# Softmax denominators of a causal attention: key blocks added by accumulating DMAs, one matmul pass of sums a unit

## The chip, the core and the metric

The kernel runs on one core of a Trainium2 chip. The metric is the device time of one execution in microseconds (us); lower is better. Engines: PE (TensorE) does matmuls, with its weight loads shown as PEld; DVE (VectorE), ACT (ScalarE) and POOL (GpSimd) do elementwise work and reductions; SP (SyncE) issues DMAs. POOL and ACT can issue DMAs too. Sixteen DMA engines move the data.

## The reference

Two residual blocks over x of 2 x 1024 tokens of 128 features, in float32. The first is causal attention with 8 query heads in 2 groups of 4, whose keys and values come from a latent of 32 per group. The second is a mixture of 32 small experts with a router. Cut to what matters:

```python
q = (xn @ wq).reshape(B, T, 2, 4, 128)
k_lat = (xn @ wk_down).reshape(B, T, 2, 32)
v_lat = (xn @ wv_down).reshape(B, T, 2, 32)
k = einsum('bkhl,ld->bkhd', k_lat, wk_up)
v = einsum('bkhl,ld->bkhd', v_lat, wv_up)
scores = einsum('bqhrd,bkhd->bhrqk', q, k) * 128 ** -0.5
scores = where(causal, scores, finfo.min)
probs = softmax(scores, axis=-1)
y = einsum('bhrqk,bkhd->bqhrd', probs, v).reshape(B, T, 1024) @ wo
x = x + layernorm(y)
x = x + layernorm(moe(layernorm(x)))
```

`moe` picks 2 of 4 expert groups for each token, then 6 experts in them, and adds a shared expert and a small anchor expert.

## The kernel before

*Attention.* Queries are multiplied by the key's up projection beforehand, so scores are products over 32 latent features, and the four heads of a group lie in the four groups of 32 partitions. The work is cut into 16 units (b, g, q): batch, group, block of `QC` = 256 queries; in order b, then q, then g. Unit q has q + 1 steps of 256 keys each (two key tiles of 128), 40 steps in all; the last step of a unit is the diagonal one (s == q), where the second key tile has only 128 queries. The main loop is in `attention()`. For step k it issues in this order:

- `numerators` (L533): scores s of the step in four PSUM banks, one for each head (L541); the maximum is subtracted by a further matmul (L555); then ACT writes the exponentials to the SBUF tile `pr` (L561: 128 keys x 4 heads x 512), and in the diagonal step POOL zeroes what lies above the diagonal (L564, affine_select). `pr` is one of three buffers with the tag "wide".
- `weigh` of the step before (k-1), which calls `values` (L574): o += v' pr on PE (L578), into the one accumulator bank with tag "o".
- `one_item`: a piece of the row maxima of a later unit, `maxima`: matmuls sm (L476, L486) in four PSUM banks and reductions on DVE (L493). Scores, maxima and the rest share seven banks that go round.
- `sums` of step k-1 (L584): a second pass of matmuls over the same `pr`, now with a matrix of ones (L587). It gives the softmax denominators in the other half of the accumulator bank. After a unit's last step ACT copies both halves to SBUF (`raw`, L594), and `normalized` divides on ACT and DVE, with a Newton step.

Between these, `tick()` lets one piece of the side work run: projections of the second batch, and `route(i)`, which takes 512 tokens whose units are normalized through the output projection, both layer norms and the router. PE, DVE, ACT, POOL and SP each run their instructions in exactly this program order.

*After attention.* `experts(0, 0)` runs all experts for the first 512 tokens. The other 1536 are sorted by expert group: POOL scatters their rows into DRAM by indirect DMAs (`placed`, L955), slots of 256 rows are worked off by `Slots.run`, and their outputs are scattered back (`results`, L1180). The experts' weights per token are spread over partitions by DMAs from DRAM (`spread_tile`, L1050, three buffers with a tag of their own; L1304 and L1310 for the first 512 tokens, issued on SP's queue).

Of the kernel before, what the change touches and what calls it, by code (L numbers as in the profile page):

```python
# [10 lines left out]
F32 = mybir.dt.float32  # L11
BF16 = mybir.dt.bfloat16
AF = mybir.ActivationFunctionType
ALU = mybir.AluOpType
# [11 lines left out]
def attn_moe_block(  # L26
# [19 lines left out]
    anchor_w_down: bass.AP,  # L46
    out: bass.AP,
):

# [64 lines left out]

    x_sb = [const.tile([P, NT, D], F32, name=f"x{b}") for b in range(B)]
    xr = [x[b].rearrange("(t p) d -> p t d", p=P) for b in range(B)]
    wq_sb = work.tile([P, NH, P], F32, tag="wide", name="wq_sb", bufs=3)
    wkup_sb = const.tile([L, P], F32, name="wkup_sb")  # L120
    wvup_sb = const.tile([L, P], F32, name="wvup_sb")
    wkd_sb = const.tile([P, G, L], F32, name="wkd_sb")
# [169 lines left out]
    def fold_queries():  # L292

        pt = bank("pt_up")
        nc.tensor.transpose(pt[:, 0:L], wkup_sb, ident[0:L, 0:L])
        nc.vector.tensor_copy(wkupT, pt[:, 0:L])
        wqT = work.tile([P, NH, P], F32, tag="wide", name="wqT", bufs=3)
        for g in range(G):
            heads = range(g * R, (g + 1) * R)
            pt = bank("pt_wq")  # L300
            for i, h in enumerate(heads):
                nc.tensor.transpose(pt[:, ts(i, P)], wq_sb[:, h, :], ident)
            nc.scalar.copy(wqT[:, g * R : (g + 1) * R, :].rearrange("p h d -> p (h d)"), pt)
            yield
        for g in range(G):
            pa = bank("pa")
            for i in range(R):
                nc.tensor.matmul(
                    pa[:, ts(i, L)], lhsT=wqT[:, g * R + i, :], rhs=wkupT, start=True, stop=True
                )  # L310
            nc.scalar.mul(aq[:, g, :], pa[:, 0 : R * L], scale)
            yield
# [219 lines left out]

    def numerators(u, s):  # L533

        b, g, q = u
        qT, kT, _ = qkv[b]
        banks = [bank(f"s{b}{g}{q}{s}") for _ in range(R)]
# [18 lines left out]
                dst, lhsT=ones[rows, :], rhs=less, start=False, stop=True, skip_group_check=True  # L556
            )
        tables(EXP_LN)
        pr = work.tile([P, R, 2 * QC], F32, tag="wide", name=f"pr{b}{g}{q}{s}", bufs=3)
        for r in range(R):  # L560
            nc.scalar.activation(pr[:, r, 0:m], banks[r][:, 0:m], AF.Exp)  # L561
        if s == q:
            own = pr.rearrange("p r (i c) -> p r i c", c=QC)[:, :, :, 0:P]
            nc.gpsimd.affine_select(  # L564
                out=own, in_=own, compare_op=ALU.is_ge, fill=0.0, base=0,
                pattern=[[0, R], [0, 2], [1, P]], channel_multiplier=-1,
            )
        return pr

# [1 line left out]

    ot = {}

    def values(u, s, pr, o):  # L574
        b, g, _ = u
        for kt, at, lo, n in pieces(u, s):
            for r in range(R):
                nc.tensor.matmul(  # L578
                    o[ts(r, L), lo : lo + n], lhsT=qkv[b][2][:, kt, ts(g, L)],
                    rhs=pr[:, r, at : at + n],  # L580
                    start=(kt == 0), stop=False, skip_group_check=True,
                )

    def sums(u, s, pr, o):  # L584
        for kt, at, lo, n in pieces(u, s):
            for r in range(R):
                nc.tensor.matmul(  # L587
                    o[ts(r, L), QC + lo : QC + lo + n], lhsT=ones32,
                    rhs=pr[:, r, at : at + n], start=False, stop=True, skip_group_check=True,
                )  # L590
        b, g, q = u
        if s == q:
            t = work.tile([P, 2 * QC], F32, tag="raw", name=f"raw{b}{g}{q}", bufs=3)
            nc.scalar.copy(t, o)  # L594
            ends.append(normalized(u, t))

    def normalized(u, t):

        b, g, q = u
        own, total = t[:, 0:QC], t[:, QC : 2 * QC]  # L600
        r = work.tile([P, QC], F32, tag="rsum", name=f"rsum{b}{g}{q}", bufs=2)
        tables(EXP_LN)
        nc.scalar.activation(r, total, AF.Ln)
        nc.scalar.activation(r, r, AF.Exp, scale=-1.0)
        yield HOP
        ot[u] = work.tile([P, QC], F32, tag="ot", name=f"ot{b}{g}{q}", bufs=NU + 2)
        nc.vector.scalar_tensor_tensor(total, total, -1.0, r, ALU.mult, ALU.mult)
        nc.vector.tensor_tensor(own, own, r, ALU.mult)
        nc.vector.scalar_tensor_tensor(ot[u], total, 2.0, own, ALU.add, ALU.mult)
        yield  # L610

    def attention():
# [31 lines left out]
        def weigh(entry):  # L644
# [3 lines left out]
            if s == 0:  # L648
                o[u] = acc(f"o{u[0]}{u[1]}{u[2]}")
            values(u, s, pr, o[u])  # L650

        for k, (u, s) in enumerate(steps):
            while done < need[k]:
# [8 lines left out]
            pr = numerators(u, s)  # L662
            if k > 5:
                tick()
            if waiting:
                weigh(waiting)
            turn_ready(ready)
# [4 lines left out]
                one_item()  # L672
            if k > 5:
                tick()
            if waiting:
                sums(*waiting, o[waiting[0]])
            waiting = (u, s, pr)
            tick()
            if any(need[j] - done > j - k - 1 for j in range(k + 1, len(steps))):
# [1 line left out]
                tick()  # L681
        weigh(waiting)
        sums(*waiting, o[waiting[0]])


    chosen = const.tile([P, NTS, NG], F32, name="chosen")
# [361 lines left out]
        return wb  # L1048

    def spread_tile(name):  # L1050
        return work.tile([P, NC * SL], F32, tag="spread", name=f"spread{name}", bufs=3)

    def quarter(name):
        return work.tile([P, QC], F32, tag="quarter", name=name, bufs=6)
# [183 lines left out]
    def finish(i):  # L1238
# [23 lines left out]
            tables(EXP_LN)  # L1262
        else:
            yield 4
        both = work.tile([P, R, 2 * QC], F32, tag="wide", name=f"y{i}", bufs=3)
        both = both.rearrange("p r c -> p (r c)")[:, 0 : n * TOPG * D]
        at = (i - ND) * TB
        nc.sync.dma_start(
# [160 lines left out]
```

## Time and profile before

| | us |
|---|---|
| timed runs of before, median of 3 | 460.58 (456.15 to 461.75) |
| profiled execution, time | 449.65 |
| profiled execution, span of its instructions | 448.0 |
| PE busy / DVE busy / ACT busy / POOL busy in the span | 402.7 / 293.2 / 220.5 / 117.5 |

The span is the time from the first to the last instruction of the profiled execution. Busy is time in which the engine has at least one instruction under way; a matmul in float32 appears as two records, and four matmuls in different quarters of the array run side by side, so a group's busy time is less than its count times its mean. A row of the page's groups gives line, engine, operation, output and input with shapes, the count, then busy time in us and the mean of one in ns, then the engine's idle time just before them and what ended it. A row of the waits gives who waited for whom: us in total, times, and the longest. In the windows, each engine's busy time stands in front of its number of instructions.

### The profile page before, as it was taken

Reading aid. Unit: us, or ns where it says so; the run is one execution under the profiler, and the core shown is the slowest. Engines: PE = TensorE matmul, PEld = TensorE weight load, DVE = VectorE, ACT = ScalarE, POOL = GpSimd, SP = SyncE. Lnnn points to the kernel's source line nnn. Section 1 sums busy time; section 2 is a strip of 40 time slices with the busy share of each in tenths; the row PEclk is TensorE's granted clock in tenths of the full one; section 3 lists DMA queues with packets and bytes.
Section 4 is the critical chain, followed back from the end, with each engine's and each line's share of the span. In section 5 each row is a group of like instructions: output and inputs, shape, how many; then the busy total and the mean of one; then the engine's idle time right before and its main releaser. Section 6 shows DMA issues by size and latency. Waiting matters only on the chain.

```text
span 448.0 us, 10253 instructions
## 1 busy us (share of the span) xinstructions
PE 402.7 (90%) x3727; PEld 253.8 (57%) x3727; DVE 293.2 (65%) x1001; ACT 220.5 (49%) x469; POOL 117.5 (26%) x296
## 2 busy tenths in 40 slices
PE   8997899999999999998998999998789999997820
PEld 4554445645555555644554544447678899986620
DVE  5469852687699789799872576597433555455734
ACT  3454376276343577565566556436323433333621
POOL 4000100020001212022001688525852334241130
PEclk9999999999999999999999999999989999999995
DMA  7888000000000620000000257677278667787221
GB/s 216 186 235 174 2 0 2 1 4 1 1 2 1 173 75 2 1 1 2 1 2 2 53 179 215 174 218 217 93 219 242 207 209 239 220 246 232 83 63 55
DMA packets 46419, 47.63 MB, mean 106 GB/s; under 512 B 21152, under 2 KB 39312, under 8 KB 46368
## 3 DMA queue, kind: packets, MB, share of 16 engines
q1 hardware_dynamic: 42960, 41.51, 33.0%
q0 software_dynamic: 2112, 4.18, 2.8%
q10 hardware_dynamic: 1296, 1.28, 0.9%
q8 instruction: 30, 0.49, 0.5%
q14 instruction: 21, 0.17, 0.1%
HBM read 38.12 MB, written 11.45 MB: 111 GB/s over the span
## 4 chain that ended last, share of the span: by engine, by line
PE 51%; DVE 22%; DMA 12%; issue 6%; ACT 5%; POOL 2%; SPq 1%; ACTq 0%; POOLq 0%; DVEq 0%
DVE nm L493 9%; PE sm L476 7%; PE s L541 5%; DMA got<-placed 5%; PE o L578 4%; PE pgs L1148 4%; PE o L587 3%; PE pus L1148 3%; PE ys L1171 3%; PE pp L429 3%; PE pg L1317 3%; DMA y<-results 2%; PE oacc L1331 2%; PE pu L1318 2%; PE po L712 2%
## 5 line engine op out<-in xcount | busy, mean ns | idle before, releaser
L493 DVE TENSOR_REDUCE nm<-sm 128x1 f32<-128x512 f32 (+2 forms) x192 | 92.7, 548 | 35.2 <-PE sm L486 24.1
L561 ACT ACTIVATE pr<-s 128x512 f32<-128x512 f32 (+1 forms) x160 | 75.6, 558 | 71.8 <-PE s L555 71.8
L564 POOL TENSOR_SCALAR_AFFINE_SELECT pr<-pr 128x1024 f32<-128x1024 f32 x16 | 18.1, 1130 | 185.9 <-ACT pr L561 185.9
L541 PE MATMUL s<-qT,kT 32*128 32x256 f32 (+1 forms) x640 | 51.1, 383 | 4.6 <-DVE nm L493 3.8
L1156 DVE TENSOR_TENSOR hids<-hids,pus 128x512 f32<-128x512 f32 x30 | 20.6, 687 | 46.4 <-PE pus L1148 44.1
L1171 PE MATMUL ys<-wd_sb,hids 128*128 x300 | 41.0, 276 | 7.1 <-DVE hids L1157 5.3
L1180 POOL DMA_INDIRECT results<-ys,to_row x30 | 31.5, 1049 | 59.6 <-ACT ys L1177 37.0
L476 PE MATMUL sm<-kT,qT 32*128 32x512 f32 (+3 forms) x384 | 46.4, 525 | 0.6 <-DVE nm L493 0.4
L1171 PEld LDWEIGHTS ys<-wd_sb,hids 128*128 128x128 f32 x300 | 40.0, 191 | 10.9 <-DVE hids L1157 6.3
L541 PEld LDWEIGHTS s<-qT,kT 32*128 32x128 f32 x640 | 33.6, 184 | 21.4 <-issue 9.8
L578 PE MATMUL o<-pr,v 128*32 128x256 f32 (+1 forms) x640 | 39.4, 364 | 1.0 <-POOL preceded L855 1.0
L587 PE MATMUL o<-pr,ones 128*32 128x256 f32 (+1 forms) x640 | 39.3, 363 | 0.0
L1148 PE MATMUL pgs<-hTp,wbs 128*128 128x256 f32 x120 | 32.0, 390 | 1.2 <-issue 1.2
L1148 PE MATMUL pus<-hTp,wbs 128*128 128x256 f32 x120 | 30.9, 380 | 0.0
L578 PEld LDWEIGHTS o<-pr,v 128*32 128x32 f32 x640 | 16.7, 109 | 22.4 <-issue 10.3
L587 PEld LDWEIGHTS o<-pr,ones 128*32 128x32 f32 x640 | 17.2, 109 | 20.0 <-issue 10.6
L1157 DVE TENSOR_TENSOR hids<-hids,spreads 128x512 f32<-128x512 f32 (+1 forms) x45 | 27.2, 604 | 1.6
L955 POOL DMA_INDIRECT placed<-rows,place_of x24 | 24.5, 1020 | 7.5 <-issue 4.5
L1155 ACT ACTIVATE hids<-pgs 128x512 f32<-128x512 f32 x30 | 17.9, 598 | 15.3 <-PE pgs L1148 15.3
L476 PEld LDWEIGHTS sm<-kT,qT 32*128 32x128 f32 x384 | 18.2, 183 | 12.4 <-issue 3.6
L1148 PEld LDWEIGHTS pus<-hTp,wbs 128*128 128x128 f32 x120 | 23.1, 192 | 3.2
L1148 PEld LDWEIGHTS pgs<-hTp,wbs 128*128 128x128 f32 x120 | 21.2, 195 | 5.0 <-issue 2.9
(303 smaller groups left out, 628.1 us busy)
## 6 DMA issues: line engine op xcount, KB each, us to landing
wbs<-wgu SPq DMA_DIRECT2D x15, 640.0 KB, 4.4
spreads<-cw_slot SPq DMA_DIRECT2D x30, 256.0 KB, 4.0
spreadd<-cw_rows SPq DMA_DIRECT2D x16, 256.0 KB
got<-placed SPq DMA_DIRECT2D x15, 180.0 KB, 3.7
placed<-zero SPq DMA_DIRECT2D x1, 2640.0 KB
wbd<-wgu SPq DMA_DIRECT2D x4, 640.0 KB, 7.2
spreads<-cw_slot SPq DMA_DIRECT2D x60, 32.0 KB, 3.5
y<-results SPq DMA_DIRECT2D x3, 512.0 KB, 3.7
```

Of the source, the lines that this page charges most:

```text
L476: nc.tensor.matmul(banks[r][:, at : at + k1 - k0], lhsT=qT[ts(r, L), g, ts(qt, P)], rhs=kT[ts(r, L), g, k0:k1], start=(at == 0), stop=Fals ...
L493: nc.vector.tensor_reduce(nm[:, k0 // BC, j, r : r + 1], banks[r][:, at : at + k1 - k0], AX.X, ALU.max, negate=True,)
L541: nc.tensor.matmul(banks[r][:, at : at + n], lhsT=kT[rows, g, ts(kt, P)], rhs=qT[rows, g, q * QC + lo : q * QC + lo + n], start=(i == 0), ...
L561: nc.scalar.activation(pr[:, r, 0:m], banks[r][:, 0:m], AF.Exp)
L578: nc.tensor.matmul(o[ts(r, L), lo : lo + n], lhsT=qkv[b][2][:, kt, ts(g, L)], rhs=pr[:, r, at : at + n], start=(kt == 0), stop=False, skip ...
L587: nc.tensor.matmul(o[ts(r, L), QC + lo : QC + lo + n], lhsT=ones32, rhs=pr[:, r, at : at + n], start=False, stop=True, skip_group_check=True,)
L955: move = nc.gpsimd.indirect_dma_start(out=placed[:, :], out_offset=bass.IndirectOffsetOnAxis(ap=place_of[:, k, t : t + 1], axis=0), in_=ro ...
L1148: nc.tensor.matmul(p[:, lo : lo + SL], lhsT=wb[:, m, ts(c, P)], rhs=hT, start=(lo == 0), stop=(c == pair[-1]), skip_group_check=True,)
L1156: nc.vector.tensor_tensor(hid[:, 0:n], hid[:, 0:n], up, ALU.mult)
L1157: nc.vector.tensor_tensor(hid[:, 0:n], hid[:, 0:n], sp[:, pair[0] : pair[-1] + 1, :].rearrange("p c t -> p (c t)"), ALU.mult,)
L1171: nc.tensor.matmul(o[:, ts(j, D)], lhsT=hid[:, at : at + P], rhs=w, start=(c == 0 and j == 0), stop=(c == NC - 1), skip_group_check=True,)
L1180: move = nc.gpsimd.indirect_dma_start(out=results[:, :], out_offset=bass.IndirectOffsetOnAxis(ap=self.to_row[i][:, j : j + 1], axis=0), in ...
```

## The change

For ten of the sixteen units (all with q > 0 except two of the last batch's second group: `by_dma`) the per-step pass of `sums` is dropped. Instead, the numerators of the unit's steps are added up in SBUF by DMAs that accumulate into their destination, issued on POOL's queue: `add_tiles` adds the first key tile's half of `pr` to the second's, `add_steps` adds the result of one step to that of the next. The matmul with ones then runs once a unit, over the total (`sums_at_once`), three steps after the unit's last one. For these additions `pr` is laid out by blocks of 128 queries: (block, head, query) instead of (head, block, query). The values' half of the accumulator is copied to SBUF as soon as the unit's last values are in, the sums' half after `sums_at_once`. The tag "wide" has six buffers instead of three, and the spread expert weights now take their buffers from it. After the change the accumulating DMAs are at L616, L618 and L623, the one pass of sums at L629, the two copies at L595 and L634, the exponentials at L565, affine_select at L570 and the values at L588.

```diff
@@ -116,7 +118,7 @@
-    wq_sb = work.tile([P, NH, P], F32, tag="wide", name="wq_sb", bufs=3)
+    wq_sb = work.tile([P, NH, P], F32, tag="wide", name="wq_sb", bufs=6)
...
@@ -556,14 +559,17 @@
                 dst, lhsT=ones[rows, :], rhs=less, start=False, stop=True, skip_group_check=True
             )
         tables(EXP_LN)
-        pr = work.tile([P, R, 2 * QC], F32, tag="wide", name=f"pr{b}{g}{q}{s}", bufs=3)
+        pr = work.tile([P, R, 2 * QC], F32, tag="wide", name=f"pr{b}{g}{q}{s}", bufs=6)
+        pr = pr.rearrange("p r c -> p (r c)").rearrange("p (k r c) -> p k r c", r=R, c=P)
         for r in range(R):
-            nc.scalar.activation(pr[:, r, 0:m], banks[r][:, 0:m], AF.Exp)
+            nc.scalar.activation(
+                pr[:, 0 : m // P, r, :], banks[r][:, 0:m].rearrange("p (k c) -> p k c", c=P), AF.Exp
+            )
         if s == q:
-            own = pr.rearrange("p r (i c) -> p r i c", c=QC)[:, :, :, 0:P]
+            own = pr[:, 0:3:2, :, :]
             nc.gpsimd.affine_select(
                 out=own, in_=own, compare_op=ALU.is_ge, fill=0.0, base=0,
-                pattern=[[0, R], [0, 2], [1, P]], channel_multiplier=-1,
+                pattern=[[0, 2], [0, R], [1, P]], channel_multiplier=-1,
             )
         return pr
 
@@ -571,33 +577,66 @@
 
     ot = {}
 
+    def by_dma(u):
+
+        return u[2] > 0 and not (u[0] == B - 1 and u[1] == G - 1 and (u[2] + 1) * QC % BC == 0)
+
     def values(u, s, pr, o):
-        b, g, _ = u
+        b, g, q = u
         for kt, at, lo, n in pieces(u, s):
             for r in range(R):
                 nc.tensor.matmul(
                     o[ts(r, L), lo : lo + n], lhsT=qkv[b][2][:, kt, ts(g, L)],
-                    rhs=pr[:, r, at : at + n],
+                    rhs=pr[:, at // P : (at + n) // P, r, :],
                     start=(kt == 0), stop=False, skip_group_check=True,
                 )
+        if s == q and by_dma(u):
+            t = raw[u] = work.tile([P, 2 * QC], F32, tag="raw", name=f"raw{b}{g}{q}", bufs=3)
+            nc.scalar.copy(t[:, 0:QC], o[:, 0:QC])
+
+    raw = {}
 
     def sums(u, s, pr, o):
         for kt, at, lo, n in pieces(u, s):
             for r in range(R):
                 nc.tensor.matmul(
                     o[ts(r, L), QC + lo : QC + lo + n], lhsT=ones32,
-                    rhs=pr[:, r, at : at + n], start=False, stop=True, skip_group_check=True,
+                    rhs=pr[:, at // P : (at + n) // P, r, :], start=False, stop=True,
+                    skip_group_check=True,
                 )
         b, g, q = u
         if s == q:
             t = work.tile([P, 2 * QC], F32, tag="raw", name=f"raw{b}{g}{q}", bufs=3)
             nc.scalar.copy(t, o)
-            ends.append(normalized(u, t))
-
-    def normalized(u, t):
-
+            ends.append(normalized(u, t[:, 0:QC], t[:, QC : 2 * QC]))
+
+    def add_tiles(u, s, pr):
+
+        if s < u[2]:
+            nc.gpsimd.dma_start(out=pr[:, 2:4], in_=pr[:, 0:2], accum_op=ALU.add)
+        else:
+            nc.gpsimd.dma_start(out=pr[:, 2], in_=pr[:, 1], accum_op=ALU.add)
+
+    def add_steps(u, s, pr, last):
+
+        own = pr[:, 2:4] if s < u[2] else pr[:, 0:3:2]
+        nc.gpsimd.dma_start(out=own, in_=last[:, 2:4], accum_op=ALU.add)
+
+    def sums_at_once(u, pr):
         b, g, q = u
-        own, total = t[:, 0:QC], t[:, QC : 2 * QC]
+        o = bank(f"sums{b}{g}{q}")
+        for r in range(R):
+            nc.tensor.matmul(
+                o[ts(r, L), 0:QC], lhsT=ones32, rhs=pr[:, 0:3:2, r, :], start=True, stop=True,
+                skip_group_check=True,
+            )
+        t = raw.pop(u)
+        nc.scalar.copy(t[:, QC : 2 * QC], o[:, 0:QC])
+        ends.append(normalized(u, t[:, 0:QC], t[:, QC : 2 * QC]))
+
+    def normalized(u, own, total):
+
+        b, g, q = u
         r = work.tile([P, QC], F32, tag="rsum", name=f"rsum{b}{g}{q}", bufs=2)
         tables(EXP_LN)
         nc.scalar.activation(r, total, AF.Ln)
@@ -648,6 +687,26 @@
             if s == 0:
                 o[u] = acc(f"o{u[0]}{u[1]}{u[2]}")
             values(u, s, pr, o[u])
+            if by_dma(u):
+                add_tiles(u, s, pr)
+
+        past = []
+
+        def add_past():
+
+            if not past:
+                return
+            u, s, pr = past[-1]
+            if by_dma(u) and s > 0:
+                assert past[-2][0:2] == (u, s - 1)
+                add_steps(u, s, pr, past[-2][2])
+
+        def sum_past():
+
+            if len(past) > 1:
+                u, s, pr = past[-2]
+                if by_dma(u) and s == u[2]:
+                    sums_at_once(u, pr)
 
         for k, (u, s) in enumerate(steps):
             while done < need[k]:
@@ -662,6 +721,7 @@
             pr = numerators(u, s)
             if k > 5:
                 tick()
+            add_past()
             if waiting:
                 weigh(waiting)
             turn_ready(ready)
@@ -672,8 +732,11 @@
                 one_item()
             if k > 5:
                 tick()
+            sum_past()
             if waiting:
-                sums(*waiting, o[waiting[0]])
+                if not by_dma(waiting[0]):
+                    sums(*waiting, o[waiting[0]])
+                past.append(waiting)
             waiting = (u, s, pr)
             tick()
             if any(need[j] - done > j - k - 1 for j in range(k + 1, len(steps))):
@@ -681,6 +744,7 @@
                 tick()
         weigh(waiting)
         sums(*waiting, o[waiting[0]])
+        assert not any(by_dma(u) for u, _, _ in past[-2:])
 
 
     chosen = const.tile([P, NTS, NG], F32, name="chosen")
@@ -1048,7 +1112,8 @@
         return wb
 
     def spread_tile(name):
-        return work.tile([P, NC * SL], F32, tag="spread", name=f"spread{name}", bufs=3)
+        t = work.tile([P, R, 2 * QC], F32, tag="wide", name=f"spread{name}", bufs=6)
+        return t.rearrange("p r c -> p (r c)")[:, 0 : NC * SL]
 
     def quarter(name):
         return work.tile([P, QC], F32, tag="quarter", name=name, bufs=6)
...
```

## The prediction

> **What bounds the kernel now.** I read the page's busy shares and slices first, then the windows, the waits, the instructions in order of time (they give each step's start), and last the DMA rows.
>
> ```profile
> PE 402.7 (90%) x3727; PEld 253.8 (57%) x3727; DVE 293.2 (65%) x1001; ACT 220.5 (49%) x469; POOL 117.5 (26%) x296
> PE   8997899999999999998998999998789999997820
> ...
> DMA  7888000000000620000000257677278667787221
> ```
>
> PE is busy in nearly every slice, and DMA is idle from 45 us to the end of attention (about 241 us), one burst apart. The windows answer splits the span there:
>
> ```profile
> 30.00:241.00 211.00, 201.33 (x2648) 108.80 (x2648) 163.00 (x620) 118.38 (x269) 22.75 (x42) 1.00 0.11 29
> 241.00:448.00 207.00, 174.38 (x876) 129.25 (x868) 114.95 (x314) 88.63 (x171) 87.45 (x208) 0.96 0.57 171
> ```
>
> The columns are PE, PEld, DVE, ACT and POOL busy, the clock, the DMA share and GB/s. In attention PE is busy for 201 of 211 us, DVE for 163, POOL for 23. The page's groups, then the waits:
>
> ```profile
> L578 PE MATMUL o<-pr,v 128*32 128x256 f32 (+1 forms) x640 | 39.4, 364 | 1.0 <-POOL preceded L855 1.0
> L587 PE MATMUL o<-pr,ones 128*32 128x256 f32 (+1 forms) x640 | 39.3, 363 | 0.0
> L1180 POOL DMA_INDIRECT results<-ys,to_row x30 | 31.5, 1049 | 59.6 <-ACT ys L1177 37.0
> ...
> PEld s L541 <- DVE nm L493: 5.6, 7, 2.4
> PE s L541 <- DVE nm L493: 3.8, 5, 2.0
> ```
>
> L587, the pass that the change attacks, holds PE for 39.3 us in 40 steps, 0.98 us a step, and waits for nothing. PE's few waits in attention are for DVE's maxima, whose PSUM banks the scores need.
>
> **What the Trainium skill says.** *Collectives: The Full Stack*, "The bandwidth ceiling: the fold count and why AG ≠ RS ≠ AR": a DMA that adds reads two sources for each write, both on the same ring, and runs at half the rate of a copy (62.28 against 32.35 GB/s on two engines). *DMA: Bandwidth & Descriptors*, "Rules for kernel authors": an accumulating DMA reads its destination and writes it later, so the next access must wait for its semaphore. This is what makes a chain here. *TensorE: Matmul & The Clock Gate*, "Part 1: The HAM clock gate": after an idle window of about 3.4 us PE runs at half clock for about as long. The trace of before has no adding DMA; it agrees on the clock, which was 0.69 in the window from 327 to 330 us, after PE was busy for only 0.96 us of the 3 us before.
>
> **The change part by part.** The 40 steps (unit, key block) are counted from 0. Some starts in order of time, by their first L541: 8 at 81.5, 20 at 143.8, 23 at 159.9, 28 at 187.5, 38 at 233.0 us.
>
> *Passes of sums.* Ten of the sixteen units (30 of 40 steps) lose L587: 30 x 0.98 = 29.5 us. Ten passes of 8 matmul records come in (L629), half of a step's 16: 5.0 us. PE has 24.5 us less to do. I count half as gained. At 99.19 us a step's maxima run on PE to 100.26; the first reduce starts at 100.34 and takes 0.62 us; the next scores start at 101.26, after the pass of sums. Of their four banks one is freed by that reduce, near 101.0. Without the pass they would start near 101.0, not 100.26. Such a step gains 0.3 us, one in which DVE is ahead gains 1.0. At -12 us PE would still have 177 us of work in 199 and DVE 163. PE alone: -12 us.
>
> *Chain of adding DMAs.* POOL issues 20 adds of 512 KB and 10 of 256 KB over key tiles (T, L616 and L618) and 20 of 512 KB over steps (S, L623). In step k its queue has S(k-2), then T(k-1). S(k-2) waits until T(k-2) and S(k-3) have landed, and T(k-1) stands behind it. PE's L629 for a unit's last step k stands in step k+3, after the maxima, and waits for S(k); the next scores, values and maxima are queued behind it. No adding DMA is in the trace, so its price has three unknown terms:
> - G, POOL's time to issue one: 1.0 us (L1180 also has 128 rows: 1049 ns). Bounds 0.5 and 1.6.
> - D, the data of 512 KB: 128 rows of 4 KB over 16 engines are 8 rows each. In the packet records of queue 0 a 4096-byte packet takes 159 ns in the median, so a copy takes 1.27 us and two reads 2.5 us. Lower end 2.0 us, an estimate from that Collectives section (32.35 GB/s on two engines); upper end 5.0 us, if the addition itself halves the rate again. I take 2.5.
> - F, the rest until the semaphore: L1180's 64 KB land 2.2 us after issue at the least and 3.5 in the median; less 1.0 for G and 0.2 for data, that is 1.0 to 2.3. I take 1.6: the queue is empty, and the target is SBUF.
>
> One add alone: 1.0 + 2.5 + 1.6 = 5.1 us. S(k-2) and T(k-1) go out together and share the engines, so from one S to the next it is G + 2D + F = 7.6 us, with a T of 256 KB 6.35. At a change of unit two T stand behind an S: G + 3D + F = 10.1. A step on PE takes about 4.5 us where nothing is fitted in between, so the chain is the longer.
>
> Batch 0: the values of step 7 end at 85.5 us before, about 4 us earlier now: 81.5. T(7) lands and S(7) goes out at 86.6. Then +6.35, +10.1, +6.35 (S(11)), +10.1, +7.6, +6.35 (S(15)), +10.1, +7.6, +6.35 puts S(19) at 157.5; it lands at 162.6. PE asks for it at the end of step 22, 159.1 before (where that step's L587 stands): +3.5 us.
> Batch 1: T(27) follows the values of step 27, 189.6 before; +3.5 from above, -2 gained since: 191.1. S(27) at 196.2, then +6.35, +10.1, +6.35, +10.1, +7.6, +6.35: S(35) at 243.1, landing at 248.2. PE asks in step 38, at 235.2 before: +13. What follows (6 us, a unit with its old pass) is unchanged. PE idles up to 10 us at such a wait, so the clock falls: +1.5. Attention ends 15 us later (14.5, rounded). The -12 is spent, since PE waits at the end of units.
>
> *Edits at nothing.* Exps into query blocks (L565), values and affine_select on such views: the same elements. Two copies of 256 columns (L595, L634) for one of 512: ten times 0.16 us (2 x 372 ns of L1177's 256 columns, less 587 of L594) on ACT, busy for 118 of 211 us. Six buffers: a pr is free after S(k+1), within three steps; fewer would add a wait. POOL's affine_select of step k stands ahead of S(k-2) but behind S(k-3); where the chain is late, that step's values wait for it instead of L629 for the DMA: the same chain, not counted twice. Normalization and routing come two steps later; the last unit keeps its old pass, so the ranking after attention keeps its place. Expert weights spread over partitions now take pr's buffers: their first loads leave SP when S(35) has landed, not at 150 us. Four DMAs (3.4 us of issue, 5.5 us to land) are then ready about 8 us after it, when the first product asks for them. This is hidden within 2 us; a later chain moves both.
>
> The stages after 241 us keep their length, and the rest of the sum stands against the profiled execution, 449.65 us with a span of 448.0: +15 gives 465. That execution lies below all three timed runs (456.15 to 461.75), so I carry the difference to their median: 460.58 + 15 = 476.
>
> **The rivals.**
> - *The passes go and the adds hide (faster).* One mechanism: in batch 1 the adds from T(27) to the landing of S(35) end before PE reaches step 38, at 224 instead of 235. They may then take 42 us; they are 14.5D + 8F + 8G. That holds from D = 1.8 at F = 1.1 and G = 1.0, or D = 2.0 if G is 0.5. For it: DMA and POOL are idle in attention. Against it: two reads a row. -12: 449.
> - *Parity.* D = 2.2 and F = 1.3 take 14.5 x 0.3 + 8 x 0.3 = 7 us off batch 1's chain and hide batch 0's 3.5: 15 - 7 - 3.5 leaves +4 or 5, within 2% of 460.6. At 2% ends about what a measurement of this kernel can tell from no change.
> - *Adding at half that rate.* Both batches have 35.5D + 19F + 19G. D = 5.0 adds 35.5 x 2.5 = 89: 565. D = 3.1 with F = 2.3 adds 21 + 13: 510. For it: nothing here shows the adder's rate.
>
> **How the numbers follow.** Chances: adds hidden, 0.16; parity, 0.22; the forecast (2% to 8% slower), 0.36; slower adds, 0.26. So slower by over 2% has 0.62, within 2% 0.22, faster 0.16. The range is 449 to 545: the low end is PE's whole gain, the high end D near 4.4; beyond it I leave a tenth.
>
> **What would show it.** Right: PE waits for DMA at L629, shortest for units of two steps and longest at the end of units of four; L629 x80 records near 5 us; POOL idle at L623 for DMA; about 5 us from issue to landing of a lone add; clock under 1.0 within attention; the stage after attention as long as before. Wrong: if lone adds land within 4 us and L629 waits for nothing, attention is shorter, DVE reduces are nearly back to back, and the fast rival holds. If S takes 8 us or more to land, the adder's rate is the bound. If attention is as predicted but the time is not, the late spread loads or the later routing have come onto the path.

## The result and the profile after

The changed kernel takes 497.44 us (494.84 to 503.84, four runs) where the kernel before takes 460.04 (456.15 to 461.75): ratio 1.080, 95% interval 1.073 to 1.088. That is 37 us slower; 476 was forecast, 15 slower. The highest of the four fell in a slower state of the core, at a lower granted clock, and the profile taken with this result is of that execution, so the ratio leaves it out and the lines here are from another run of the same kernel (`again` below), with a span of 494.7 us. The two profiles differ by 46.7 us and not by 37, in part because that of before is of an execution 11 us under its median. First the page of the changed kernel: engines, slices, groups and DMA issues.

```profile
PE 413.3 (84%) x3327; PEld 260.1 (53%) x3327; DVE 295.8 (60%) x1001; ACT 222.1 (45%) x479; POOL 163.2 (33%) x346
PE   8998999968687879896976489999969999998740
...
PEclk9998699979787889998897599999998999999995
DMA  8995265484777663348588661926827776787312
...
L544 PE MATMUL s<-qT,kT 32*128 32x256 f32 (+1 forms) x640 | 66.6, 437 | 7.8 <-DVE nm L495 7.7
...
L588 PE MATMUL o<-pr,v 128*32 128x256 f32 (+1 forms) x640 | 45.7, 410 | 0.7 <-POOL preceded L919 0.7
L623 POOL DMA_DIRECT2D pr<-pr x20 | 20.7, 1034 | 66.8 <-DMA pr<-pr 62.8
...
L629 PE MATMUL sums<-pr,ones 128*32 128x256 f32 x80 | 8.6, 510 | 27.7 <-DMA pr<-pr 26.6
...
pr<-pr POOLq DMA_DIRECT2D x40, 512.0 KB, 5.1
```

The row of the scores before, which L544 is to be compared with, was:

```profile
L541 PE MATMUL s<-qT,kT 32*128 32x256 f32 (+1 forms) x640 | 51.1, 383 | 4.6 <-DVE nm L493 3.8
```

There are 400 fewer matmul records on PE than before, and yet PE's busy time rose from 402.7 to 413.3 us: the clock row has 6s to 8s within attention (up to slice 23 of 40), and the means of L544 (437 ns, before 383) and L588 (410, before 364) are longer. DMA is now busy throughout attention, and PE waits 26.6 us at L629 for the additions. An addition of 512 KB takes 5.1 us from issue to landing in the median. The windows, with the columns of before (length, then PE, PEld, DVE, ACT and POOL, clock, DMA share, GB/s), put the loss in one place:

```profile
30.00:287.00 257.00, 211.49 (x2276) 114.70 (x2272) 165.60 (x620) 121.49 (x283) 70.50 (x94) 0.86 0.61 116
287.00:494.00 207.00, 174.38 (x872) 129.30 (x864) 114.91 (x314) 88.42 (x171) 86.24 (x208) 0.96 0.58 169
```

What follows attention takes 207 us as before, with the same 174.38 us of PE. Attention ends at 287 instead of 241.6. The waits (who for whom, us in total, times, longest):

```profile
POOL pr L623 <- DMA pr<-pr: 62.8, 13, 7.4
...
PE sums L629 <- DMA pr<-pr: 26.6, 5, 11.1
```

POOL waits for the DMAs before it issues the next addition over steps (L623), and PE waits for them before the pass of sums (L629). The instructions in order of time show how the two waits feed each other. POOL first, then one line of PE and two of ACT:

```profile
122.35 1.20 POOL L623 DMA_DIRECT2D pr<-pr  x1 [5.11 <-DMA pr<-pr]
123.07 2.29 POOL L616 DMA_DIRECT2D pr<-pr  x2
133.37 1.09 POOL L570 TENSOR_SCALAR_AFFINE_SELECT pr<-pr 128x1024 f32<-128x1024 f32 x1 [8.00 <-ACT pr L565]
134.41 0.86 POOL L623 DMA_DIRECT2D pr<-pr  x1
```

```profile
127.60 1.08 PE L629 MATMUL sums<-pr,ones 128*32 128x256 f32 x8 [5.13 <-DMA pr<-pr]
129.65 1.67 PE L544 MATMUL s<-qT,kT 32*128 32x256 f32 x16
```

```profile
128.73 0.37 ACT L634 COPY raw<-sums 128x256 f32<-128x256 f32 x1 [5.05 <-PE sums L629]
131.65 1.64 ACT L565 ACTIVATE pr<-s 128x384 f32<-128x384 f32 x4 [1.65 <-PE s L558]
```

The addition issued at 122.35 lands, and L629 starts at 127.60; only then come the next scores (129.65), their exponentials (131.65) and their affine_select (133.37), and that stands on POOL's queue ahead of the next addition over steps, at 134.41. From one to the other are 12.1 us; the prediction has 10.1.

### The profile page after: what moved, and what is told of

Read it like the earlier page. It is cut to its first block, busy times and chain, and to the rows that moved or that the text cites. A ratio compares the mean times of both kernels' runs of the same rounds, so it can differ in the third digit from the quotient of the medians.

```text
span 501.6 us, 9588 instructions
## 1 busy us (share of the span) xinstructions
PE 412.6 (82%) x3327; PEld 260.7 (52%) x3327; DVE 296.6 (59%) x1001; ACT 222.2 (44%) x479; POOL 162.5 (32%) x346
## 4 chain that ended last, share of the span: by engine, by line
PE 47%; DMA 24%; DVE 11%; issue 8%; POOL 3%; ACT 3%; SPq 2%; POOLq 0%; ACTq 0%; DVEq 0%
DMA pr<-pr 14%; PE s L544 6%; PE sm L478 4%; DVE nm L495 4%; PE o L588 4%; PE ys L1236 3%; PE pg L1382 3%; PE pgs L1213 3%; PE pus L1213 3%; PE pu L1383 3%; PE oacc L1396 3%; PE pp L431 3%; DMA y<-results 2%; DMA got<-placed 2%; DMA cw_slot<-cwTs 2%
## 5 line engine op out<-in xcount | busy, mean ns | idle before, releaser
L565 ACT ACTIVATE pr<-s 128x512 f32<-128x512 f32 (+1 forms) x160 | 75.8, 561 | 75.3 <-PE s L558 74.3
L544 PE MATMUL s<-qT,kT 32*128 32x256 f32 (+1 forms) x640 | 66.0, 432 | 7.7 <-DVE nm L495 7.5
L544 PEld LDWEIGHTS s<-qT,kT 32*128 32x128 f32 x640 | 43.5, 209 | 29.8 <-DVE nm L495 11.4
L570 POOL TENSOR_SCALAR_AFFINE_SELECT pr<-pr 128x1024 f32<-128x1024 f32 x16 | 19.1, 1197 | 95.1 <-ACT pr L565 95.1
L478 PE MATMUL sm<-kT,qT 32*128 32x512 f32 (+3 forms) x384 | 47.5, 557 | 1.8 <-DVE nm L495 1.6
L588 PE MATMUL o<-pr,v 128*32 128x256 f32 (+1 forms) x640 | 44.0, 398 | 1.0 <-POOL preceded L919 1.0
L623 POOL DMA_DIRECT2D pr<-pr x20 | 20.7, 1033 | 68.2 <-DMA pr<-pr 61.0
L629 PE MATMUL sums<-pr,ones 128*32 128x256 f32 x80 | 9.0, 535 | 28.3 <-DMA pr<-pr 27.1
L588 PEld LDWEIGHTS o<-pr,v 128*32 128x32 f32 x640 | 17.8, 116 | 26.1 <-issue 17.7
L558 PE MATMUL s<-mT,ones 32*128 32x512 bf16 (+1 forms) x160 | 25.5, 386 | 3.7 <-DVE mT L526 3.7
L616 POOL DMA_DIRECT2D pr<-pr x20 | 22.7, 1218 | 14.6 <-PE pm L522 8.3
L1387 DVE TENSOR_TENSOR hid<-hid,pu 128x512 f32<-128x512 f32 x20 | 13.7, 685 | 20.4 <-PE pg L1382 9.6
L478 PEld LDWEIGHTS sm<-kT,qT 32*128 32x128 f32 x384 | 18.2, 192 | 13.3 <-issue 2.6
```

The lines of the kernel that those rows point to most:

```text
L478: nc.tensor.matmul(banks[r][:, at : at + k1 - k0], lhsT=qT[ts(r, L), g, ts(qt, P)], rhs=kT[ts(r, L), g, k0:k1], start=(at == 0), stop=Fals ...
L544: nc.tensor.matmul(banks[r][:, at : at + n], lhsT=kT[rows, g, ts(kt, P)], rhs=qT[rows, g, q * QC + lo : q * QC + lo + n], start=(i == 0), ...
L558: nc.tensor.matmul(dst, lhsT=ones[rows, :], rhs=less, start=False, stop=True, skip_group_check=True)
L565: nc.scalar.activation(pr[:, 0 : m // P, r, :], banks[r][:, 0:m].rearrange("p (k c) -> p k c", c=P), AF.Exp)
L588: nc.tensor.matmul(o[ts(r, L), lo : lo + n], lhsT=qkv[b][2][:, kt, ts(g, L)], rhs=pr[:, at // P : (at + n) // P, r, :], start=(kt == 0), s ...
L616: nc.gpsimd.dma_start(out=pr[:, 2:4], in_=pr[:, 0:2], accum_op=ALU.add)
```

## The experiments

### The unaltered kernel, and PE kept warm

Each ratio is to runs of the kernel before that were made with the experiment on the same chip; their median was 453.6 to 460.7 us, so between groups of experiments the ratios can be compared and the times cannot.

`again` is the changed kernel as it is. `warm` puts filler matmuls (the kernel's `awake` helper) ahead of the pass of sums, so that PE does not idle there.

> The changed kernel unaltered, for a second profile. Both theories: a ratio of 1.07 to 1.09 to the kernel before; L629 waits for DMA about 25 us in all; half clock for about 60 us within attention; the stage after attention as long as before (207 us).

```diff
     def sums_at_once(u, pr):
         b, g, q = u
+        if q > 1:
+            awake(24)
         o = bank(f"sums{b}{g}{q}")
```

> 24 filler matmuls (L320) stand ahead of L629 in the seven units with more than two steps, so that PE is not idle for the first 5 to 6 us of its wait for the adds. Clock theory (the wait halves PE's clock, and the slow PE feeds the chain of adds late): half clock in attention falls from about 60 us to under 25, and the kernel gains 10 to 20 us, to a ratio near 1.045. Theory of the DMA chain alone, as in the prediction: the chain sets the pace whatever PE's clock, so within 4 us of the changed kernel (ratio 1.07 to 1.09), or slower by the filler in the units whose wait was under 5 us.

`again`: 494.31 us, ratio 1.090 (1.078 to 1.101). `warm`: 501.66 us, ratio 1.101 (1.090 to 1.113) on the same chip. The waits at the pass fell from 26.6 to 9.0 us and the time at half clock within attention from 71.7 to 34.1 us, but attention ended at 289.7 instead of 287.3. This does not separate the clock from the rest, because the fillers took 39.0 us of PE themselves (168 matmuls at L320), also ahead of the two passes for which PE had not waited (235.5 and 251.0 us in `again`). Ahead of the second of these they held PE for 5.3 us, and the next addition over steps left 16.2 us after the one before it, where it was 11.1. What the lower clock costs stays open after this run.

### The pass of sums a step later; the additions ahead of affine_select; both

```diff
# late_sums
-            if len(past) > 1:
-                u, s, pr = past[-2]
+            if len(past) > 2:
+                u, s, pr = past[-3]
# add_first
+            add_past()
             pr = numerators(u, s)
             if k > 5:
                 tick()
-            add_past()
# first_late: both
```

> L629 stands one step later (four steps after the unit's last). DMA chain alone: the adds take as long as before, so the last one of batch 1 lands at the same time and PE gains at most the 3 to 4 us of a step's slack: ratio 1.07 to 1.085. Theory of the loop through PE (PE's wait at L629 holds back the numerators, and with them the affine_select that stands ahead of the next add on POOL): waits at L629 shrink by a step's 4 to 5 us each, the clock stays up, and 15 us or more come back: ratio 1.05 or less.

> The adds over steps of step k-2 are issued ahead of step k's numerators, so on POOL they stand ahead of its affine_select. Loop through PE: the intervals between adds at changes of unit fall from 11 to 13 us to about 10, and 6 to 10 us come back (ratio 1.06 to 1.07). DMA chain alone: those intervals are made of data and landing, so no change (ratio 1.075 to 1.085).

> Step additions ahead of the new step's numerators (affine_select then stands behind them on POOL's queue) and the pass of sums one step later, both together. Loop theory (the pass waiting on TensorE holds back the exponentials, these affine_select, this the next addition): the two edits cut the loop at two places, so together they gain less than their sum, 7 + 16 us: ratio 1.03 to 1.05, the L629 waits under 13 us, and the spacing of step additions at the bare transfers, 7.6 us and 6.35 within a unit, 10.1 at its change. If they act on separate losses: 1.02 to 1.03. If a rate of the transfers alone sets the pace, no less than the 1.0565 of the later pass alone.

`late_sums`: 478.25 us, 1.057 (1.049 to 1.064); attention ends at 266.3, waits at L629 are 12.3 us. `add_first`: 487.93 us, 1.073 (1.064 to 1.081); attention ends at 278.6, and the spacing at a change of unit is 10.8 to 11.4 us where it was 11.1 to 13.1. Each lies between its two expectations. Each opens the loop and takes part of the loss away, 16 and 6.4 us against `again`. But `first_late`, 489.1 us, 1.063 (1.058 to 1.067), is no better than the later pass alone: it misses the 1.03 to 1.05 that the loop alone would give, and is what was expected if the transfers alone set the pace. Its attention ends at 271.6, and its waits say where the gain went:

```profile
POOL pr L623 <- DMA pr<-pr: 72.6, 14, 7.8
...
PEld o L588 <- POOL pr L570: 13.2, 7, 5.4
...
PE o L588 <- POOL pr L570: 10.2, 6, 5.1
PE sums L629 <- DMA pr<-pr: 7.7, 1, 7.7
```

With the addition ahead of it on POOL, affine_select waits for the DMA, and PE's values (L588) wait for affine_select: 13.2 us of weight loads and 10.2 of matmuls here, 2.6 and 1.2 in `late_sums`. The wait has moved from the pass to the values. What remains in both kernels is a spacing close to the prediction's bare chain (6.35 to 7.6 us, and 10.1 at a change of unit): in `late_sums` 6.4 to 9.2 us within a unit and 10.8 to 11.9 at its change.

### What is left without the additions

```diff
# no_adds: neither addition is issued
-                add_tiles(u, s, pr)
+                pass
...
-                add_steps(u, s, pr, past[-2][2])
+                pass
# no_steps: only the second of these
# none_by_dma: no unit is summed by DMA
-        return u[2] > 0 and not (u[0] == B - 1 and u[1] == G - 1 and (u[2] + 1) * QC % BC == 0)
+        return False
```

> Both kinds of additions are left out (the denominators then miss most of the numerators); layout, six buffers, copies and the one pass of sums a unit stay. It is the ceiling of the change: what the saved TensorE passes give if adding costs nothing. The prediction's sum, 24.5 us less for TensorE of which half is gained, gives 448 us where before takes 460: ratio 0.96 to 0.98. If the loss stems from the additions and what waits for them, it comes out there or lower, and the half-clock time within the attention returns to 0 to 5 us. If layout, copies or buffers cost time of their own, it stays at 1.00 or above.

> Only the additions over steps (L623) are left out (denominators then hold the last step alone); those over key tiles stay, 30 of them. Chain theory: what costs is that each step's addition waits for the one before; the tile additions have no successor to wait for, so the ratio falls to within 0.015 of the kernel without any additions, 0.96 to 0.99, and L629 hardly waits. If traffic itself costs (POOL's issues at 1.2 us each, the queues' packets at 338 ns, numerators held longer), half of the loss stays: 1.03 to 1.05.

> No unit is summed by DMA: sums run step by step on TensorE as before, over the new layout of numerators by query blocks, with six buffers and the late weights in them. The prediction costed all of this at nothing: ratio 1.00, within 0.01. If the strided writes of the exponentials and the strided reads of the two passes cost time (in the changed kernel the values took 44.0 us where they took 39.4), the ratio is 1.02 to 1.03 and the scalar engine's exponentials or the values' matmuls are longer in their means.

`no_adds`: 460.15 us, 1.001 (0.999 to 1.003). `no_steps`: 461.95 us, 1.003 (1.000 to 1.006). `none_by_dma`: 459.73 us, 0.995 (0.993 to 0.998). This splits the loss. The layout, the six buffers and the late weights cost nothing. The 30 additions over key tiles cost nothing by themselves (`no_steps`). All of the loss appears when the additions over steps join them. And the TensorE passes, once dropped, bring nothing even where no addition is made (`no_adds`): the ceiling of the change is no gain. I had expected 0.96 to 0.98 here.

The windows of `none_by_dma` and of `no_adds` (same layout, with and without the passes), and their matmul groups in this stretch, show where the saved work went:

```profile
31.50:244.00 212.50, 203.35 (x2657) 109.59 (x2656) 163.13 (x620) 118.68 (x270) 23.23 (x44) 0.99 0.13 29
```

```profile
L544 PE MATMUL s<-qT,kT 32*128 32x256 f32 (+1 forms) x608 | 50.0, 388 | 4.6 <-DVE nm L495 3.8 <-DVE mT L526 0.8
...
L602 PE MATMUL o<-pr,ones 128*32 128x256 f32 (+1 forms) x640 | 39.3, 363 | 0.0
...
L558 PE MATMUL s<-mT,ones 32*128 32x512 bf16 (+1 forms) x152 | 18.3, 361 | 0.3 <-DVE mT L526 0.3
```

and without the passes:

```profile
31.50:244.00 212.50, 194.51 (x2240) 107.55 (x2236) 163.68 (x619) 119.86 (x279) 22.63 (x43) 0.95 0.12 28
```

```profile
L544 PE MATMUL s<-qT,kT 32*128 32x256 f32 (+1 forms) x608 | 61.6, 400 | 9.8 <-DVE nm L495 9.7
...
L558 PE MATMUL s<-mT,ones 32*128 32x512 bf16 (+1 forms) x152 | 24.4, 368 | 3.7 <-DVE mT L526 3.7
L602 PE MATMUL o<-pr,ones 128*32 128x256 f32 (+1 forms) x148 | 8.7, 349 | 0.0
L629 PE MATMUL sums<-pr,ones 128*32 128x256 f32 x80 | 6.4, 390 | 0.0
```

The passes shrank from 39.3 to 15.1 us (8.7 + 6.4), 24.2 us less, just as counted. The scores L544 grew by 11.6 us and L558 by 6.1, though the mean of one hardly changed: they overlap less; PE's idle time before L544 grew by 5.2 and before L558 by 3.4. The scores of step 12 in order of time, first with the pass, then (all engines) without:

```profile
105.61 1.14 PE L478 MATMUL sm<-kT,qT 32*128 32x512 f32 x8
106.68 0.86 PE L602 MATMUL o<-pr,ones 128*32 128x256 f32 x16
107.47 1.17 PE L544 MATMUL s<-qT,kT 32*128 32x256 f32 x16
```

```profile
104.02 1.14 PE L478 MATMUL sm<-kT,qT 32*128 32x512 f32 x8
...
104.99 1.85 PE L544 MATMUL s<-qT,kT 32*128 32x256 f32 x15
...
105.18 2.48 DVE L495 TENSOR_REDUCE nm<-sm 128x1 f32<-128x512 f32 x4
105.93 0.51 PEld L544 LDWEIGHTS s<-qT,kT 32*128 32x128 f32 x9 [0.38 <-DVE nm L495]
...
106.68 0.37 PE L544 MATMUL s<-qT,kT 32*128 32x256 f32 x1
```

With the pass, the 16 score matmuls run in one go behind it and end 3.0 us after the maxima began (108.64 less 105.61). Without it they start at once, but must wait within their group for banks that DVE's reduces free: nine weight loads wait for the first reduce (0.62 us from 105.18) and run at 105.93, and the last matmul starts at 106.68, after the second. It ends 3.0 us after the maxima began, too. So 0.86 us of work went and no time. The pass of sums had lain in the time of those reduces: it filled a wait.

A rival is the clock, which was 0.95 in `no_adds` and 0.99 with the passes. It is not the main cause: from the values of step 7 to those of step 18 both ran at full clock, and that took 54.6 us without the passes and 55.5 with them. By step 30 the kernel without passes was 4.9 us ahead (values at 200.2 against 205.1 us; 1.0 of it from the start), and it lost this before step 36 (233.2 and 233.4). There, two stretches of 3.4 us at half clock can have cost 3.4 us at most (an estimate: half of their length), and PE waited 3.37 us for the last unit's maxima from DVE:

```profile
229.26 0.61 PE L558 MATMUL s<-mT,ones 32*128 32x512 bf16 x4 [3.37 <-DVE mT L526]
```

### The maxima moved ahead of the values

If the wait for the reduce is what ate the gain, putting the values between maxima and next scores might cover it.

```diff
+            if done < len(items):
+                one_item()
             if waiting:
                 weigh(waiting)
             turn_ready(ready)
             tick()
-            if done < len(items):
-                one_item()
```

> No additions by DMA (denominators incomplete), and within a step the maxima now stand ahead of the values instead of behind them. Score bank theory: without the pass of sums nothing is left between the maxima and the next scores, and these must wait until VectorE's reduce (2.48 us for four) frees their last bank, so that the 24 us saved come back as stretched and waiting L544 and L558. With the values between, that wait is covered: attention ends at 226 to 236 instead of 244, ratio to before 0.965 to 0.985. If the step's round through exponentials and reduces has a length of its own, the wait only moves (to the maxima's fourth bank, behind the first exponential): ratio 0.99 to 1.01.

> All sums on TensorE step by step as before, new layout, and the maxima ahead of the values in each step. TensorE is busy for 203 of 212 us there, so the order can gain little: ratio within 0.01 of the 0.995 of the same kernel with the order of before. Below 0.985 the gain of the exchange would be its own, not that of the saved passes; above 1.01 the exchange itself costs.

`no_adds_swap`: 468.69 us, 1.033 (1.026 to 1.039). `none_swap`: 476.5 us, 1.047 (1.040 to 1.054). Both are slower: the exchange itself costs, which I had not expected of either, so it is no clean test of the wait for the reduce; that stays read from the traces. In `no_adds_swap` the maxima are now the group that stretches:

```profile
L478 PE MATMUL sm<-kT,qT 32*128 32x512 f32 (+3 forms) x336 | 70.6, 560 | 1.9 <-ACT pr L565 1.5
L544 PE MATMUL s<-qT,kT 32*128 32x256 f32 (+1 forms) x588 | 51.3, 416 | 7.7 <-DVE nm L495 7.7
```

L478 takes 70.6 us instead of 43.7: its weight loads wait for the exponentials (L565) 31 times, 17.3 us in all. So a step's way through scores, exponentials, maxima and reduces has a length of its own, and PE's wait in it moves with the order. In this worse order dropping the passes does bring something, 1.4 points of the ratio; in the kernel's own order they lie where they cost nothing.

### Half of the units

```diff
# half_late, on top of first_late
-        return u[2] > 0 and not (u[0] == B - 1 and u[1] == G - 1 and (u[2] + 1) * QC % BC == 0)
+        return u[2] > 0 and u[1] == 0
...
-            if len(past) > 2:
-                u, s, pr = past[-3]
+            if len(past) > 3:
+                u, s, pr = past[-4]
...
         weigh(waiting)
+        sum_past()
```

> Only the six units of group 0 with q > 0 are summed by DMA, those of group 1 step by step on TensorE; step additions ahead of the numerators, the pass of sums two steps later. The units alternate, so a chain of additions (7.6 us a step) has the steps of two units to run in. Chain theory: additions fit, L629 waits under 3 us in all, and the time is that without additions: ratio 1.00, within 0.015. If each addition costs by its traffic, POOL issue or held buffers, 12 of 20 step additions leave half of the loss: 1.04 to 1.05.

465.01 us, 1.024 (1.018 to 1.029): between the two expectations. The additions did fit: L629 waits 1.3 us in all, and attention ends at 247.0, 3 us after `no_adds`. Most of the 11 us by which the kernel is slower lies behind attention, and I read it as a cost of this edit's own order. Its last pass of sums (of the unit that ends with step 35) now stands behind the loop, at 244.7 us, and the ranking follows late:

```profile
261.46 0.18 PE L965 MATMUL ranka<-mba,before 128*128 128x32 bf16 x1
```

That is 14.4 us after the end of attention, where it is 6.3 in `no_adds` (250.4) and in `again`; POOL's first scatter of rows comes 32.9 us after it instead of 24.9. So about 8 us belong to the place of that pass. This is read from the traces and was not tried.

### What about the additions costs: bytes, or the dependence between them

```diff
# half_bytes: 64 of the 128 partitions
-            nc.gpsimd.dma_start(out=pr[:, 2:4], in_=pr[:, 0:2], accum_op=ALU.add)
+            nc.gpsimd.dma_start(out=pr[0:64, 2:4], in_=pr[0:64, 0:2], accum_op=ALU.add)
...
-        nc.gpsimd.dma_start(out=own, in_=last[:, 2:4], accum_op=ALU.add)
+        nc.gpsimd.dma_start(out=own[0:64], in_=last[0:64, 2:4], accum_op=ALU.add)
# half_cols: one of two blocks in every partition
-            nc.gpsimd.dma_start(out=pr[:, 2:4], in_=pr[:, 0:2], accum_op=ALU.add)
+            nc.gpsimd.dma_start(out=pr[:, 2], in_=pr[:, 0], accum_op=ALU.add)
...
-        nc.gpsimd.dma_start(out=own, in_=last[:, 2:4], accum_op=ALU.add)
+        nc.gpsimd.dma_start(out=pr[:, 2], in_=last[:, 2], accum_op=ALU.add)
# unchained: the step before is read as it was before any addition
-        nc.gpsimd.dma_start(out=own, in_=last[:, 2:4], accum_op=ALU.add)
+        nc.gpsimd.dma_start(out=own, in_=last[:, 0:2], accum_op=ALU.add)
```

> The changed kernel with each addition over partitions 0 to 63 only (the other half of the partitions is not added): all waits, the order on POOL's queue and the number of additions stay, the bytes are half. By the prediction's prices the data term of an addition falls from 2.5 to 1.25 us and issue and ends stay: within a unit 7.6 becomes 5.1, at its change 10.1 becomes 6.4, close to the 4.8 us in which TensorE makes a step. If the length of the transfers carries the loss, the ratio is 1.01 to 1.035 and L629 waits under 10 us. If the round through the waits themselves carries it (a pass of sums, exponentials, affine_select, next addition, each behind the other), it stays at 1.06 or above.

> All 128 partitions, but half of each partition's bytes: each addition takes one of the two blocks of 128 queries (so half of the numerators is not added). Waits, order and number of additions as in the changed kernel. Over half of the partitions the bytes of an addition halved but its transfer did not (2.8 us as before), so that run could not tell. Here a 2048-byte packet took 186 ns against 338, so the transfer should fall to 1.4 us: within a unit 7.6 becomes 6.2, at its change 10.1 becomes 7.5 or less. If the length of the transfers carries the loss: ratio 1.02 to 1.045. If the round through the waits carries it: 1.06 or above, with L629 waiting 15 us or more.

> Additions of the same number, size, place on POOL's queue and destination, but each step addition reads the raw numerators of the step before (its first key tile) instead of that step's running sum, so that no addition waits for the previous step's; the last one still waits for its own step's numerators and tile addition. Denominators then hold two steps only. Chain theory (each step's addition must wait for the one before, and the pass of sums for all of them): ratio 0.99 to 1.02, L629 waits under 8 us. If the bytes, POOL's issues at 1.0 to 1.2 us or the buffers held carry the loss, it stays above 1.05.

`half_bytes`: 487.07 us, 1.073 (1.065 to 1.081). This looked like a verdict for the waits, but the packet records show that it halved nothing that mattered: 64 packets of 4096 bytes took 658 ns each where 128 had taken 338, so a lone addition's data still lasted 2.8 us. `half_cols` has the same bytes in total, over all partitions, and its packets of 2048 bytes take 185 ns in the median: 467.39 us, 1.019 (1.012 to 1.027). Attention ends at 250.1, and POOL's additions stand closer:

```profile
128.81 0.86 POOL L623 DMA_DIRECT2D pr<-pr  x1 [5.05 <-DMA pr<-pr]
129.35 1.21 POOL L618 DMA_DIRECT2D pr<-pr  x1
...
134.18 0.86 POOL L623 DMA_DIRECT2D pr<-pr  x1 [3.32 <-DMA pr<-pr]
```

5.4 us from one to the next here, 5.1 to 6.8 within units; in `again` 6.4 to 9.2. The same number of waits, POOL issues and additions thus costs 2% instead of 8 or 9 when the transfer is shorter. The bytes in all do not decide it, since `half_bytes` has as few, and neither does the clock alone: it was 0.92 within attention in `half_bytes` and 0.86 in `again`, with a loss nearly as large. `unchained` took 494.45 us, 1.075 (1.066 to 1.084): no addition over steps reads another one's result any more, and the loss is all there.

```profile
113.35 0.86 POOL L623 DMA_DIRECT2D pr<-pr  x1
113.91 1.18 POOL L618 DMA_DIRECT2D pr<-pr  x1
121.14 1.20 POOL L623 DMA_DIRECT2D pr<-pr  x1 [6.05 <-DMA pr<-pr]
```

The spacing is no shorter, 7.8 us here. I read the reason from these rows: L618, the addition over key tiles of the next step, is issued 0.6 us after L623 into the same DMA engines, and the next L623 writes into the tile that this L618 fills, so it must wait for it anyway. Two transfers in a row per step are the period, whether or not the sums are chained.

No version here goes clearly below the kernel before. `none_by_dma`, 0.995 (0.993 to 0.998), is the best, and it makes no use of the additions.

## Why the prediction was right or wrong

**Direction, place and prices: right.** Attention carries the whole loss, and the stage after it has its 207 us. The additions over steps land 4.6 to 5.7 us after their issue, where 5.1 was summed from G = 1.0, D = 2.5 and F = 1.6; the data of a lone 512 KB last 2.8 us, a little more than D; POOL's rows are 1034 ns for L623 and 1201 for L616, and the packets of 4096 bytes take 338 ns against 159 for a copy. The Trainium skill's statement in *Collectives: The Full Stack*, "The bandwidth ceiling: the fold count and why AG ≠ RS ≠ AR", that an adding DMA reads twice and moves at half the rate of a copy, agrees with this factor of 2.1 (the page measured it for collectives in a ring of four ranks, not for additions within one core). The rival of a still slower adder (565 us) is out. The fast rival's first condition was misreckoned: D = 1.8, F = 1.1 and G = 1.0 give 42.9 us, not 42 or less; nothing else hangs on it.

**"I count half as gained ... PE alone: -12 us": wrong, nothing was gained.** `no_adds` gained nothing, 1.001. The prediction read a right step, at 99.19 us, and saw that a score bank hangs on the reduce, but it counted the first bank only. In step 12 the last score matmul runs after the second reduce, and what comes behind it (the exponentials, the next maxima) moves as a whole. Of 24.2 us taken off PE, about 4 had been gained by step 30, and none reached the end of attention.

**"The same chain, not counted twice": wrong.** The prediction let affine_select of step k stand ahead of S(k-2), and costed that at nothing, because values and L629 would only wait at different places for the same DMA. But affine_select comes at the end of a line that starts at L629: the pass waits for the DMA, the scores for the pass, the exponentials for the scores, affine_select for them, and the next addition for it. So a late landing delays the next issue: 11.1 to 13.1 us at the changes of unit instead of 10.1; the bare chain itself takes 10.8 (`add_first`, three times). Step 7's addition was issued at 95.8 us (predicted 86.6), step 19's at 176.4 (157.5), step 27's at 220.6 (196.2), step 35's at 273.1 (243.1), and attention ended at 287 instead of 256. The first 9 us were lost ahead of step 7's addition: 4 are a gain of PE that the sum took as made, 2 a later start of this profile.

The chain had taken 4 us of PE's gain in batch 0 and 2 in batch 1. Without them its own sum gives about +20 instead of +15 (an estimate from the prediction's terms). `late_sums` opens the line at the pass; it takes 24.6 us more than before, and `again`, on the same chip, 40.7. So of the loss about 15 us were forecast, 6 are the gain that did not come, and 16 are what opening this line took back, with whatever the clock has in it; on that chip 4 are left over. That is a sum of single runs; the parts need not add exactly, as `first_late` shows.

**"The clock falls: +1.5": the term was too small, its cost not shown.** Half clock lasted 71.7 us within attention (20.5 already in `no_adds`), and L629's mean of 510 ns against 390 in `no_adds` goes with it. `warm` took away half of it and won nothing, but its fillers cost time of their own. That a slower PE mostly fills its own wait here, since the chain of additions sets the pace, is my reading and is not shown.

**Waits at L629.** In `again` 4.1 and 5.1 us in the first batch's units of three steps, none in the second batch's, 2.6 and 3.7 in the first batch's units of four, 11.1 at the last one, none for an addition in units of two. The last was put at up to 10 and is nearly right; in batch 0 the prediction had 3.5 in all and there were 15.5. L629 itself took 8.6 us, not 5.0: 6.4 even without the additions, and the rest comes with the lower clock.

**Edits at nothing: right.** Layout, six buffers and late weights: 0.995. The weights' first loads left SP from 265 us on, around the last addition (273.1), and no product waited for them.

## What to carry to other kernels

Before a pass is priced as saved, ask what lies beside it: here the sums on PE filled the time in which VectorE freed the next scores' banks, so that "busy for 201 of 211 us" did not make them worth anything. A replacement of the pass by a transfer is then judged by one figure, its period on its own engine against the step's: 7.6 us by the sum, and 6.4 to 9.2 measured, in a step of about 5 us (210 us of attention in 40 steps); with 5.1 to 6.8 us (`half_cols`) 2% were still lost. And if the engine that waits for the transfer also feeds the queue that issues the next one, the delays are added and not overlapped: follow each queue once around before costing such a wait at nothing.

## What the hardware showed that was not expected

Adding half of the bytes was clearly faster only where each partition's part was halved. Over 64 partitions instead of 128, with the same 4096 bytes in each, a packet took 658 ns instead of 338 and the whole addition 2.8 us as before; over 128 partitions with 2048 bytes each, a packet took 185 ns. So in these runs the length of an addition followed the bytes of a partition and not the bytes in all. Why was not tried.
